# Re-ordering the stretch between two images in a two-layer state-space kernel: loads of x, token copies, first scalings, decays and planner ranks

## The chip, the cores and the metric

The kernel runs on one core of a Trainium2 chip, as one launch. The metric is the device time of that launch in microseconds (us), where less is better. Three runs of the kernel before gave 22851.89, 22874.44 and 22874.82 us, so the median is 22874.44 us.

## The reference, cut to what matters

The input is eight images of 64 x 64 positions with 192 channels, float32. Two residual layers follow each other. Layer 0 is a convolution, a chunked state-space block and an MLP; the change leaves its code alone. Layer 1 is what the change is about:

```
x = x + L1(groupnorm(x))
L1:  xz = x @ in_proj.T ; xc, z = split(xz)                 # 192 -> 2 x 384 channels
     xc = silu(depthwise_conv3x3(xc) + b)
     xs = [rows, columns, rows reversed, columns reversed]  # K = 4 directions, L = 4096 steps each
     dt, B, C = split(x_proj @ xs) ; delta = softplus(dt_proj @ dt + bias)
     h[t] = exp(delta*A) * h[t-1] + (delta*u) * B           # 384 channels x 16 states
     y[t] = sum_n h[t] * C ; y += D * xs
     y = layernorm(sum of the four directions) * silu(z) ; out = y @ out_proj.T
```

## The kernel before, in words

Layer 0 runs over all eight images first. Layer 1 then runs image by image. One image has two parts.

**The scan** (`main`, L1891) is the long part. It takes 32 steps (4 directions x 8 chunks of 512 tokens), and each step has 24 units (8 pairs of states x 3 channel tiles of 128). A unit needs `ea` (ScalarE's exponentials of the decay, `decay`, L1735, read from `dr`, the repeated delta), `g` (TensorE's transposes of `pw`, `supply`, L1747, where `pw` is ScalarE's scaling of `duT` by B, `weigh`, L1720), two VectorE scans (`run`, L1775) and GpSimd's product with `cb`, the repeated C. TensorE sums `hs` into `y` (L1813), and VectorE adds `y` to `yacc` once per channel tile and step (L1824). For the state pairs from p = 4 on, the first 128 columns of `g` are not transposed from `pw` but multiplied with `dg`, a diagonal matrix that is built in DRAM: a small strided write into `dz` (L1624) and then a load of `dg` (L1625). The order of pairs is 0, 4, 1, 5, ..., so the fourth unit of an image is the first that needs `dg`.

**The boundary** between two images does three things at once. It finishes the image that was just scanned (`finish`, L1354): mean and variance by TensorE (`p_m`, `p_v`, L1366), centring (L1378) and scaling (L1423) on VectorE, the gate `z` (reload x as `xa2`/`xb2`, multiply with the scaled weights `wza`/`wzb`, silu, product at L1498), the output projection `p_o` (L1517, L1529), the addition to x (L1543) and the store. The four token groups of x go through two buffers of `xa2`/`xb2`, so the third and the fourth group can only be loaded once the first and second have been stored. It also prepares the next image (`front`, L1157): load x as `xa1`/`xb1` in four groups, project it (`p_x`, L1150 and L1151), copy it into a bordered tile `pad` (L1215), convolve with nine taps in 3 channel tiles x 2 halves (ScalarE the first tap, `begin`, L1241; VectorE the other eight, `convolve`, L1257, 48 instructions of 128 x 2048), silu, and store three layouts: `xo0` by rows (L1282), `xo1` by columns through the transposing copy `xt` (L1296, L1303), and `xo2` by tokens (`by_tokens`, L1309: TensorE transposes `p_xq`, copies `xq`, stores). Last comes the prologue of the next scan (`prologue`, L1839, and `prologue_of`, L1873): load the first chunk `xc` and `ut` (L1591, L1595), project it (`p_d`, L1610), copy to `xdbl` (L1617), softplus (`spa`, L1652), `de` (L1658), the repeated `dr` (L1709), `duT` (L1674), ten first scalings `pw` and two first decays `ea`.

The nine boundaries (before the first image, seven between images, after the last) are not written out by hand. Each is planned by `Flow` (L105): generators yield steps with an engine, a cost and an earliest start; `Flow.run` always takes the step with the smallest planned start plus 0.01 x the rank of its generator (`RANKS`, L43), and `Flow.keep` ties each engine's instructions to the order so found. So costs and ranks in the text are not times: they decide in which order each engine issues. The order on an engine is then fixed. TensorE, VectorE, ScalarE and the DMA queue of SyncE each work it off in that order, and a waiting instruction holds what stands behind it. In the built program each DMA issue also waits for the landing of the DMA eight places before it in SyncE's queue.

Of the kernel before, what the change touches and what calls it, by code (L numbers as in the profile page):

```python
# [40 lines left out]
BIG = 60.0  # L41

RANKS = dict(  # L43
    begin=-31, fill=-131, enter=-89, load=-44, store=-81, convolve=-1, prologue=-61, project=-11, product=-20, norm=-22,
    square=-24, silu=-131, centre=-36, gate=-94, weights=285, drift=8,
)
# [1000 lines left out]
def layer1(tc, consts, x1s, mv1, out, w_in, w_x, w_dt, w_out):  # L1047
# [7 lines left out]
    with ExitStack() as ctx:  # L1055
# [67 lines left out]
        def scaled(wa, wb, b, half):  # L1123

            cols = slice(half * DIN, half * DIN + DIN)
            load = lambda: [
                nc.sync.dma_start(out=wa, in_=w_in[:C1, cols]),
                nc.sync.dma_start(out=wb[:C2], in_=w_in[C1:, cols]),
                nc.sync.dma_start(out=wb[C2:], in_=w_in[C1:, cols]),
            ]  # L1130
            r = yield step("SP", 0.3, load)
            r += 3
            for w, g in ((wa, sca), (wb, scb)):
                r = yield step(
                    "ACT", 0.5, lambda: [nc.scalar.activation(w, w, AF.Copy, scale=g[:, b : b + 1])], r
                )
            return r
# [19 lines left out]
        def front(f, cx, cx2, mq, b, xo):  # L1157
# [19 lines left out]
            def enter():  # L1177
                yield from scaled(wxa, wxb, b, 0)
                for d in range(DT):
                    for g in range(NG):  # L1180
                        yield "wait", ("xl", g)
                        ps = []
                        for i in range(2):
                            yield "take", "mm"
                            ps.append(mq.tile([128, TT], F32, name="p_x1", tag="mm"))
                        got["ps", d, g] = ps
                        f.at["ps", d, g] = yield step(
                            "PE", 2.6, lambda: from_pair(ps, wxa, wxb, xas[g], xbs[g], slice(d * 128, d * 128 + 128))
                        )
# [57 lines left out]
            def convolve():  # L1247
                for d in range(DT):
                    for h in range(2):
                        yield "wait", ("begun", d, h)  # L1250
                        xs, r = got["xs", d, h], f.at["begun", d, h]
                        for j in range(1, 9):
                            r = yield step(
                                "DVE",
                                2.24,
                                lambda: [
                                    nc.vector.scalar_tensor_tensor(  # L1257
                                        xs, tap(d, h, j), kw[:, d, j : j + 1], xs, ALU.mult, ALU.add
                                    )
                                ],  # L1260
                                r - f.LAG,
                            )
                        f.at["conv", d, h] = r
                    f.give("pad", r)
# [5 lines left out]
            def store():  # L1270
                for d in range(DT):
                    yield "take", "xt"
                    xt = gp.tile([128, WI, HI], F32, name="xt1")
                    for h in range(2):
# [14 lines left out]
                        if h == 0:  # L1289
                            seeded(q + 3)  # L1290
                        f.fork(by_tokens(d, h, xs, r))
                        r = yield step(
                            "ACT",
                            3.7,
                            lambda: [
# [13 lines left out]
            def by_tokens(d, h, xs, r):  # L1309
                xf = xs.rearrange("p h w -> p (h w)")  # L1310
                for e in range(2):
# [31 lines left out]
                    q = yield step("SP", 0.1, lambda: [nc.sync.dma_start(out=dst, in_=xq)], q)  # L1343
                    f.give("xq", q + 3)
                    if g == 0:
                        seeded(q + 3)
# [7 lines left out]
        def finish(f, cx, mq, b):  # L1354
# [62 lines left out]
            def scale(t, yv, rs, r):  # L1417
                for d in range(DT):
                    r = yield step(
                        "DVE",  # L1420
                        0.62,
                        lambda: [
                            nc.vector.scalar_tensor_tensor(  # L1423
                                yv[:, d], yv[:, d], v["gam"][:, d : d + 1], rs, ALU.mult, ALU.mult
                            )
                        ],
                        r - f.LAG,
                    )
# [3 lines left out]

            def load(gs):
                for g in gs:
                    yield "take", "xl2"
                    xa = fp.tile([C1, 2, TT], F32, name="xa2", bufs=2)
                    xb = fp.tile([128, TT], F32, name="xb2", bufs=2)
                    got["xl2", g] = xa, xb
                    r = yield step("SP", 0.3, lambda: pair_of(xa, xb, x1s[b], g))
                    f.at["xl2", g] = r + 3  # L1440

            def weights():
                f.at["wz"] = yield from scaled(wza, wzb, b, 1)

            def gate(gs):
                yield "wait", "wz"
                for g in gs:
# [3 lines left out]
                    for d in range(DT):  # L1451
# [3 lines left out]
                        for i in range(2):  # L1455
# [4 lines left out]
                            "PE",  # L1460
                            2.6,
                            lambda: from_pair(ps, wza, wzb, xa, xb, slice(d * 128, d * 128 + 128)),
# [24 lines left out]
            def product(gs):  # L1487
                for g in gs:
                    yield "rank", RANKS["product"] + g * RANKS["drift"]
                    yield "wait", ("ln", g)  # L1490
                    for d in range(DT):
# [3 lines left out]
                            "DVE",  # L1495
                            1.15,
                            lambda: [
# [51 lines left out]

            ts, gs = range(NT), range(NG)  # L1550
            gens = (project(gs), product(gs), norm(ts), square(ts), silu(gs), centre(ts), gate(gs), weights(), load(gs))
            return [(gen, RANKS[gen.__name__]) for gen in gens]

# [10 lines left out]
        def scan(xo):  # L1564
# [154 lines left out]

            def weigh(s, p, j, i):  # L1720

                st = state[s]
                if i == 0:
                    st["pw", p, j] = pools["pw1"].tile([128, 2 * DT, 2, 64], F32, name="pw")
                n = 2 * p + i
                o(
                    nc.scalar.activation(  # L1727
                        st["pw", p, j][:, :, i],
                        st["duT"][:, j].rearrange("p (g c) -> p g c", c=64),
                        AF.Copy,  # L1730
                        scale=st["bt"][:, j, n : n + 1],
                    )
                )

# [104 lines left out]
            def prologue(f, mq, cx_b, cx_a):  # L1839
# [23 lines left out]
                for name, n in (("pw1", 8), ("bc1", 3), ("e1", 3)):  # L1863
                    spool(name, n)
                load_c(0, ORDER[0])
                for d in range(DT):
                    yield "wait", ("du", d)
                for t in todo[:10]:
                    yield step("ACT", 0.55, lambda: weigh(*t), f.free["ACT"])
                for u in range(2):  # L1870
                    yield step("ACT", 1.35, lambda: decay(u), None, "explog")

            def prologue_of(f, d):  # L1873
# [8 lines left out]
                f.give("tmp", r)  # L1882
                yield step("SP", 0.1, lambda: repeat_delta(0, d), r)
                yield "take", "mm"
# [40 lines left out]
            def chains(f, mq, cx_b, cx_a):  # L1925
                f.pool("tmp", 2)
                return [(prologue(f, mq, cx_b, cx_a), RANKS["prologue"])] + [
                    (prologue_of(f, d), RANKS["prologue"]) for d in range(DT)
                ]
# [3 lines left out]
        for b in range(nb + 1):  # L1933

            f = Flow(tc, after=True)
            f.STAY = 0.0
            keeper.append(f.keep)
            mq_x, fr_x, fq_x, fi_x = ExitStack(), ExitStack(), ExitStack(), ExitStack()
# [123 lines left out]
```

## Time and profile before

| what | value |
|---|---|
| median of three runs | 22874.44 us |
| the profiled execution: its own time, its span | 22840.11 us, 22838.4 us |
| busy share of the span: TensorE, VectorE, ScalarE, GpSimd | 94%, 93%, 87%, 70% |
| mean granted TensorE clock | 0.976 |
| first scan of the first image starts; last scan of the eighth ends | 4958.7 us; 22715.2 us |
| seven boundaries between last and first scan, each | 212.1, 212.2, 215.7, 216.7, 212.9, 215.3, 218.9 us |
| stretch after the last scan | 123.2 us |

The view of stretches gives, for each window of the execution (us from the span's start), each engine's busy time with its number of instructions, then the granted TensorE clock, the mean busy share of the 16 DMA engines and the rate in GB/s. The timeline lists instructions in order of time: start, duration, engine, line, operation, output<-inputs, shape, how many were merged, and in brackets how long the engine was idle just before, and whose end it waited for. SPq is SyncE issuing a DMA; its duration is the issue and not the transfer. A line of the view of waits names who waited for whom, the total, how often, and the longest.

### The profile page before, as it was taken

How to read it: one execution, taken by the hardware profiler on the slowest of the kernel's cores; microseconds unless marked ns; L12 is line 12 of the kernel's file. 1: busy time of each engine (PE TensorE's matmuls, PEld its weight loads, DVE VectorE, ACT ScalarE, POOL GpSimd, SP SyncE). 2: the span in 40 equal slices, each digit the busy share in tenths (PEclk: the TensorE clock that was granted, in tenths of full speed). 3: DMA queues.
4: the chain of work that ended last, by engine and by line, in shares of the span. 5: the costliest groups of instructions: out<-in, count | busy, mean ns of one | idle time of the engine just before them, and what ended most of it. 6: DMA issues, size and time to landing. Idle time of an engine off the chain costs nothing.

```text
span 22838.4 us, 348211 instructions
## 1 busy us (share of the span) xinstructions
PE 21469.6 (94%) x118788; PEld 10895.2 (48%) x118788; DVE 21138.2 (93%) x22413; ACT 19918.9 (87%) x35288; POOL 16095.4 (70%) x12872
## 2 busy tenths in 40 slices
PE   8999999979999999999989999999999999999999
PEld 4444444435554555455545554554455445544554
DVE  7888888869998999899989998999899999999998
ACT  6666666669998999899989998999899989988998
POOL 1111111139995999599959995999599869987997
PEclk8999999989999999999999999999999999999999
DMA  2111111133333333333333333333333333333333
GB/s 53 46 45 42 46 46 46 39 89 92 93 93 109 93 93 95 106 92 95 93 108 93 94 89 111 92 96 85 114 93 93 88 114 93 93 85 114 93 93 79
DMA packets 1706715, 1954.31 MB, mean 86 GB/s; under 512 B 538112, under 2 KB 1039776, under 8 KB 1695712
## 3 DMA queue, kind: packets, MB, share of 16 engines
q1 hardware_dynamic: 1704928, 1932.03, 31.2%
q8 instruction: 933, 15.29, 0.3%
q14 instruction: 854, 7.00, 0.1%
HBM read 1316.16 MB, written 212.60 MB: 67 GB/s over the span
## 4 chain that ended last, share of the span: by engine, by line
PE 47%; ACT 24%; DVE 10%; POOL 8%; issue 5%; DMA 4%; SPq 2%; DVEq 0%; POOLq 0%; ACTq 0%
ACT ea L1742 11%; ACT pw L1727 10%; PE y L1813 10%; PE g L1768 10%; POOL hs L1798 7%; DVE hs L1784 3%; PE g L1756 3%; PE p_f L970 3%; PE p_d L1610 2%; PE p_x L463 2%; PE p_f L990 2%; DMA dr<-de 2%; PE p_dt L1645 2%; PE p_o L887 2%; PE p_y L804 1%
## 5 line engine op out<-in xcount | busy, mean ns | idle before, releaser
L1798 POOL TENSOR_TENSOR hs<-hs,cb 128x1024 f32<-128x1024 f32 x6144 | 14577.3, 2373 | 501.7 <-DMA dr<-de 5.6
L1784 DVE TENSOR_TENSOR_SCAN hs<-ea,cy,g 128x512 f32<-128x512 f32 x10752 | 12900.7, 1260 | 186.2 <-PE g L1768 167.2
L1742 ACT ACTIVATE ea<-dr,an 128x512 f32<-128x512 f32 x12288 | 8140.7, 710 | 431.2 <-DVE hs L1784 399.8
L1727 ACT ACTIVATE pw<-duT,bt 128x384 f32<-128x384 f32 x14336 | 7833.5, 601 | 15.9 <-DVE duT L1674 15.9
L1813 PE MATMUL y<-hs,sel 128*64 128x512 f32 x24576 | 6632.6, 618 | 357.5 <-POOL hs L1798 338.2
L1768 PE MATMUL g<-ident,pw 128*128 128x128 f32 x43008 | 6094.4, 281 | 50.6 <-DVE hs L1784 13.4
L1768 PEld LDWEIGHTS g<-ident,pw 128*128 128x128 f32 x43008 | 4612.4, 141 | 2533.8 <-issue 1232.4
L1796 POOL COPY cy<-hs 128x2 f32<-128x2 f32 x6144 | 1151.6, 187 | 1979.0 <-DVE hs L1784 1933.4
L1756 PEld LDWEIGHTS g<-dg,duT 128*64 128x64 f32 x24576 | 1556.5, 136 | 2065.9 <-issue 1493.8
L1756 PE MATMUL g<-dg,duT 128*64 128x128 f32 x24576 | 2257.8, 282 | 180.6 <-DVE hs L1784 106.2
L1813 PEld LDWEIGHTS y<-hs,sel 128*64 128x64 f32 x24576 | 1234.2, 135 | 1559.2 <-issue 869.4
L1784 DVE TENSOR_TENSOR_SCAN hs<-ea,g 128x512 f32<-128x512 f32 x1536 | 1751.9, 1198 | 149.5 <-PE g L1768 93.9
L380 POOL TENSOR_TENSOR s<-xs 96x512 f32<-96x512 f32 x64 | 116.3, 1817 | 2130.4 <-DVE xs L358 1841.7
L1257 DVE SCALAR_TENSOR_TENSOR xs<-pad,p,xs 128x2048 f32<-128x2048 f32 x384 | 900.1, 2349 | 150.2 <-ACT xs L1241 141.3
L1645 PE MATMUL p_dt<-xdbl,wd 13*128 13x512 f32 x1536 | 865.1, 644 | 98.0 <-DVE duT L1674 71.8
L1610 PE MATMUL p_d<-xc,wx 128*44 128x512 f32 x1536 | 796.9, 602 | 73.2 <-DMA xc<-xo 73.2
L380 POOL TENSOR_TENSOR s<-sq 96x512 f32<-96x512 f32 x128 | 182.5, 1426 | 938.5 <-ACT sq L393 822.6
L970 PE MATMUL p_f<-h,wf 96*128 96x512 f32 x1536 | 757.0, 631 | 43.9 <-ACT zs L565 27.4
L358 DVE SCALAR_TENSOR_TENSOR x<-xx,p,x 96x512 f32<-96x512 f32 x1024 | 783.8, 815 | 15.2 <-ACT x L347 15.0
L358 DVE SCALAR_TENSOR_TENSOR xs<-xin,p,xs 96x512 f32<-96x512 f32 x1024 | 746.7, 769 | 3.6 <-ACT xs L347 3.6
L990 PE MATMUL p_f<-m,wf 128*96 128x512 f32 x1536 | 692.9, 601 | 0.0
L1667 PEld LDWEIGHTS p_du<-ident,de 128*128 128x128 f32 x3072 | 322.7, 141 | 610.5 <-DVE de L1658 408.8
(213 smaller groups left out, 19352.5 us busy)
## 6 DMA issues: line engine op xcount, KB each, us to landing
cb<-cd SPq DMA_DIRECT2D x4096, 128.0 KB
dr<-de SPq DMA_DIRECT2D x3072, 128.0 KB
xc<-xo SPq DMA_DIRECT2D x256, 768.0 KB
dg<-dz SPq DMA_DIRECT2D x256, 512.0 KB
e<-csd SPq DMA_DIRECT2D x256, 384.0 KB
ut<-xo SPq DMA_DIRECT2D x128, 768.0 KB
ut<-xo SPq DMA_DIRECT2D x256, 384.0 KB
xo<-xs SPq DMA_DIRECT2D x48, 1024.0 KB
```

Source lines behind the costliest of these rows:

```text
L358: nc.vector.scalar_tensor_tensor(im(out[:, ct]), tap(ct, j), w[:, ct, j : j + 1], im(out[:, ct]), ALU.mult, ALU.add)
L970: nc.tensor.matmul(ps, wf1[:, ct, mt * 128 : mt * 128 + 128], h[:, ct], start=ct == 0, stop=ct == 1)
L1610: nc.tensor.matmul(st["p_d"][:44], wx[:, d, k], st["xc"][:, d], start=d == 0, stop=d == DT - 1)
L1645: nc.tensor.matmul(ps, st["wd"][32:45, d * 128 : d * 128 + 128], xds[s % 2][32:45], start=True, stop=True)
L1727: nc.scalar.activation(st["pw", p, j][:, :, i], st["duT"][:, j].rearrange("p (g c) -> p g c", c=64), AF.Copy, scale=st["bt"][:, j, n : n + 1],
L1742: nc.scalar.activation(ea[:, f], state[s]["dr", d][:, f], AF.Exp, scale=an[:, k, p, at : at + 1])
L1756: nc.tensor.matmul(gs[f][i * 64 : i * 64 + 64, j * 128 : j * 128 + 128], state[s]["duT"][:, j, (2 * d + f) * 64 : (2 * d + f) * 64 + 64], ...
L1768: nc.tensor.transpose(gs[f][:, j * 128 : j * 128 + 128], state[s]["pw", p, j][:, 2 * d + f].rearrange("p a b -> p (a b)"), ident,)
L1784: nc.vector.tensor_tensor_scan(rev(h[:, f]), rev(ea[:, f]), rev(g[f]), 0.0 if first(s) else state[s - 1]["cy"][:, p, d, f : f + 1], ALU.mu ...
L1796: o(nc.gpsimd.tensor_copy(st["cy"][:, p, d], h[:, :, last]))
L1798: o(nc.gpsimd.tensor_mul(h, h, bc(st["cb", p], 1, [128, 2, TT])))
L1813: o(nc.tensor.matmul(y[half[f]], sel, hc[:, f], start=p == ORDER[0] and k > 0, stop=p == ORDER[-1]))
```

## The change

The planner's numbers change (`RANKS` for every generator; the costs of `p_x` and `p_z` steps 2.6 to 2.95, a tap 2.24 to 2.36, and small ones). Beyond that:

```diff
+DRAIN = 8.5, 9.0
 # scaled():
-            r += 3
+            r = max(r, DRAIN[0] * half) + 3
 # store(): the column copy waits until the first token store of its half is planned
                         f.fork(by_tokens(d, h, xs, r))
+                        yield "wait", ("tokens", d, h)
                         r = yield step("ACT", 3.75, ... nc.scalar.copy(xt...) ...)
 # by_tokens():
                     f.give("xq", q + 3)
+                    if e == 0:
+                        f.at["tokens", d, h] = q
 # finish(): load() becomes fetch(), and it and weights() wait for the front's last load of x
+                    if b < nb - 1:
+                        yield "wait", ("xl", NG - 1)
-                    f.at["xl2", g] = r + 3
+                    f.at["xl2", g] = max(r, DRAIN[0]) + 3
 # weigh() can run on VectorE
+                if vector:
+                    o(nc.vector.tensor_scalar_mul(to, what, by))
+                else:
+                    o(nc.scalar.activation(to, what, AF.Copy, scale=by))
 # prologue(): four of the first ten scalings go to VectorE, the two first decays get a chain of their own
-                for t in todo[:10]:
-                    yield step("ACT", 0.55, lambda: weigh(*t), f.free["ACT"])
+                for n, t in enumerate(todo[:10]):
+                    if n < 8 and t[3]:
+                        yield step("DVE", 0.5, lambda: weigh(*t, True), at)
+                    else:
+                        yield step("ACT", 0.55, lambda: weigh(*t), at)
+            def prologue_decays(f):
+                yield "wait", "spools"
                 for u in range(2):
+                    yield "wait", ("dr", u)
                     yield step("ACT", 1.35, lambda: decay(u), None, "explog")
 # the boundary's planner
             f.STAY = 0.0
+            if b:
+                f.free["PE"], f.free["DVE"] = DRAIN
```

The scan's own loop is the same. The instructions of a boundary are the same in number and kind, but for the four scalings that change engine and for fewer switches of ScalarE's function table; their order on each engine is another.

## The prediction

> **What bounds the kernel now.** I read the page first (VectorE and TensorE are 93% and 94% busy, so a mean says little), then the stretches. The code that changes runs only in the boundaries:
>
> ```profile
> core 0: us, PE busy (x) PEld busy (x) DVE busy (x) ACT busy (x) POOL busy (x), PEclk, DMA share, GB/s
> ...
> 11475.20:11690.90 215.70, 182.87 (x536) 71.84 (x536) 169.05 (x116) 133.90 (x146) 6.25 (x9) 0.92 0.44 142
> ...
> 22715.20:22838.40 123.20, 115.24 (x300) 43.43 (x300) 55.16 (x59) 47.34 (x57) 5.42 (x5) 0.96 0.19 55
> 4790.00:4958.70 168.70, 76.15 (x259) 41.69 (x258) 119.28 (x67) 86.74 (x91) 1.79 (x5) 0.66 0.52 164
> ```
>
> Seven such boundaries, the first and the last make 1796 us, 8% of the span. In a middle one VectorE works 169 of 216 us, so about 47 us are to be had, and no more. To see where they are I read VectorE's timeline of the boundary at 11475, counting from T = 11482.8, where TensorE's last `y` ends:
>
> ```profile
> 11482.91 0.69 DVE L1824 TENSOR_TENSOR yacc<-yacc,y 128x512 f32<-128x512 f32 x1 [2.77 <-PE y L1813]
> ...
> 11507.93 23.79 DVE L1257 SCALAR_TENSOR_TENSOR xs<-pad,p,xs 128x2048 f32<-128x2048 f32 x10 [15.89 <-ACT xs L1241]
> ...
> 11628.10 33.26 DVE L1257 SCALAR_TENSOR_TENSOR xs<-pad,p,xs 128x2048 f32<-128x2048 f32 x14
> ...
> 11672.29 0.68 DVE L1617 COPY xdbl<-p_d 44x512 f32<-44x512 f32 x1 [6.36 <-PE p_d L1610]
> ...
> 11690.90 1.22 DVE L1784 TENSOR_TENSOR_SCAN hs<-ea,g 128x512 f32<-128x512 f32 x1 [2.63 <-DMA xo<-xq]
> ```
>
> The taps begin at T+25 and end at T+178.5, VectorE being nearly full between; the first chunk is in `xdbl` from T+189.5; the scan starts at T+208. The start is late because of SyncE:
>
> ```profile
> SPq L1146 <- PE y L1813: 17.5, 1, 17.5
> ```
>
> The first load behind `wxb` is `xa2` of the finishing image, whose memory is freed by the last `y`. It waits 17.5 us, and the loads of the next image's x stand behind it; the one that the first taps need is the fifth pair of six.
>
> The first scan is not the end of the boundary. The fourth unit waits for `dg`:
>
> ```profile
> 11702.56 1.12 PE L1756 MATMUL g<-dg,duT 128*64 128x128 f32 x8 [8.16 <-DMA dg<-dz]
> ```
>
> so it scans only at 11704.56 (T+221.7), after 5.48 us of idle VectorE. From there on nothing depends on the boundary: in each of the seven, the 25th unit follows the fourth by 58.8 to 59.4 us. So I measure a boundary by its fourth unit. Read alike in all seven timelines, the means are: taps T+25.8 to T+177.7, `xdbl` T+187.1, first scan T+207.2, fourth unit T+219.6 (215.2 to 223.1).
>
> **What the Trainium skill says.** "DMA: Bandwidth & Descriptors", section "Issuing engines are not separate DMA queues": all DMAs share the same 16 engines. The trace agrees: from 11673 to 11703 their mean share is near 0.9 at 200 to 437 GB/s, so order decides what lands when. Its section "Two DMAs through the same engine are not ordered" has a dependent DMA issued only after the first one's semaphore; here `dg` waits for `dz` (3.4 us where nothing else is in the way, 11718.77). "TensorE: Matmul & The Clock Gate", section "What's actually happening": after an idle window of about 3.4 us TensorE runs at half clock; the trace grants 0.50 at 11667, and `p_d` costs 3.61 + 1.10 us there, twice its warm price. "ScalarE: Activation LUTs", section "What ACT_TABLE_LOAD costs": 1283 ns plus a drain; the trace has 1.28 us.
>
> **The change, part by part,** for a middle boundary, in the order that the built program issues.
>
> *Loads of x first.* The four pairs follow `wxb` at once; what they wait for is work of the scan long done. So they issue from 11465.4. 3.1 MB at the 270 GB/s of 11486 to 11501 is 12 us plus some 2 of latency, so they land by 11480, behind the last products. Then TensorE sets the start: a cold group (3.57 + 1.12 = 4.7, as at 11496.96) and two of 2.97 give T+10.7. But ScalarE's queue now has the scaling of `wza` and `wzb` between the first group's pads and the second's. The last boundary has just this order of loads, and its scalings start at 22732.72 and 22733.65, T+9.9 and T+10.8; they are done at T+11.4. Behind them stand four pads of 0.63 and the first tap's 2.1: T+16.1 instead of 25.8, 9.7 us earlier. Without the scalings it would be T+14.2, so this wait costs 1.9.
>
> *Two centrings moved.* Before, two of 1.7 us ran in the idle start; now the first comes after nine taps. That is 3.4 us more between the first and the last tap; all other counts up to the last tap stay (48 taps, 18 scalings, 9 products, 6 additions). The stretch was 151.9 us, idle included, and becomes 155.3. I walked the queues for new idle: TensorE runs all twelve `p_x` groups early, which fills the eight PSUM banks, and ScalarE waits with the third tile's pads for tap 16; but five centrings' means are ready when VectorE asks. One product waits about 3 us for the third reload of `xa2`, as large as the waits it replaces (4.92 at 11551.7). Taps end at T+171, 6.7 us earlier. Bounds: 0 to 10 earlier.
>
> *Tokens ahead of the column copy.* The first chunk needs `xo0` and the first token store of the third tile. Their transposes stand on TensorE behind `p_z` of the fourth group, whose `xa2` is stored and reloaded (8.6 us at 11597.49, 12.2 at 11625.61 with `xo1` in front). The last addition before it falls at T+145, so `p_z` starts at 154 to 157; 3 us, two transposes, two copies, the 3.8 us column copy, two more copies and the store bring the load of `xc` to T+166. It lands 8.1 later (11658.28), and a cold `p_d` of 4.7 gives `xdbl` at T+178, 9.1 us earlier.
>
> *From `xdbl` to the fourth unit* was 32.5 us. Now three products (1.2 each) stand before `de`, and the column copy (3.8) has moved between the second and third softplus, so the third `de` comes about 13.5 us after `xdbl` instead of 8.5. More important, SyncE's order ends with eight `dr`, `xo1`, three stores, `xo2`, two `cb`, four `dr`, three stores, and only then `dz` and `dg`; before, `dz` was ahead of `cb`. The bytes from `dr` to the last store are 1.05 + 2.1 + 0.79 + 0.52 + 0.26 + 0.52 + 0.79 = 6.0 MB. At 280 GB/s with `xo1` at 437 that is 19 us; `dr` begins 8 us after `xdbl`, add 1.7 of latency and 1 for slow issue: 30. `dg` lands 5 later, and TensorE needs 2: 37 us, 4.5 more than before. The first boundary, which has `dz` last already, took 32.2 with 1.5 MB less (5.4 us): 37.6. So the fourth unit comes at T+215, a gain of 4.6.
>
> *First scalings and decays.* Ten scalings took ScalarE 5.17 us. Six take 3.1; VectorE's four cost 0.40 each (128x192 takes 0.30, 128x128 0.27); bounds 0.27 to 0.69. The first scan may start 6 to 10 us earlier, but it is followed by the wait for `dg`, so I count nothing; if `dg` were early, some 3 us.
>
> *Table loads.* ScalarE switches four times less, 5.1 us; it is not the bound, so zero. If it were late at the third softplus, one switch would be worth 1.3.
>
> *First boundary:* the end is the same `dr`, `dz`, `dg`; `xc` is earlier, but its use waits for the last tap: 1 us gained (0 to 3). *Last:* TensorE is 115 of 123 us busy and does the same work; `ysq` now stands behind the scalings, and a product ends nearer the end: 1 us lost (-2 to 4).
>
> Sum: 7 x 4.6 + 1 - 1 = 32 us. The profiled execution of 22840.1 becomes 22808. The median lies 34 us above that execution, and the runs scatter by 23, so I carry the difference over: 22874.4 - 32 = 22842.
>
> **Rivals.** *The whole head start arrives.* If `dg` lands 32.5 us after `xdbl` as before, each boundary gains 9.1, 64 us: 22811. For it: 30 us of the DMA's work is an estimate. Against: `dz` last. *The end swallows it.* If the end takes 41.6 us, the gain is nil: 22874; the same comes if the loads don't issue early, against which the built waits speak. *Slower:* SyncE's queue at the end, with place and price: the 6.0 MB run at 0.19 MB/us instead of 0.28 (199 and 215 GB/s stand at 11685 to 11691, where `dr` and `cb` with their small rows dominate), and `xo1` loses its higher rate. Then they take 31.6 us instead of 19, the end 49.6 and a boundary 8.0 us more: 7 x 8.0 = 56, 22930. It turns the sign from an end of 41.6 us on.
>
> **How the numbers follow.** Forecast 0.42, whole gain 0.30, swallowed 0.18, slower 0.10. A change under 0.2% (46 us) is about what a measurement here can't tell from none. Faster than that: 0.26 from the whole gain, 0.15 from the forecast's upper part, 0.41; slower 0.08, from the last; the same 0.51. The range goes from 84 us faster (12 per boundary, all bounds of the start well used) to 16 us slower, 22790 to 22890; the forecast's own is 22815 to 22865. Both sides of the sign lie in it because seven repeated ends multiply each us of error.
>
> **What would show it.** Right: loads of `xa` issued some 17 us before the last `y` ends; first tap near T+16 behind ScalarE's scalings; last tap near T+171; `xdbl` near T+178; first scan near T+198; VectorE idle over 10 us before the fourth unit, released by `dg`, at T+215. Wrong: taps interrupted by idle TensorE or ScalarE stretches, or `dg` landing within 33 us of `xdbl`, or beyond 42.

## The result, and the profile after

| | median | lowest to highest | runs |
|---|---|---|---|
| kernel before | 22859.61 us | 22838.03 to 22878.45 | 11 |
| kernel after | 22806.38 us | 22793.09 to 22824.09 | 11 |

The ratio is 0.9977, with a 95% interval of 0.9968 to 0.9986: 53 us faster, 0.23%, with 32 to 73 in the interval. The three runs that the prediction starts from had a median 15 us above the one that stands here.

The profiled execution of the kernel after took 22798.87 us, with a span of 22797.2 and a mean TensorE clock of 0.975. The view of stretches, for the same three stretches as before (the middle boundary is now at T = 11485.8):

```profile
core 0: us, PE busy (x) PEld busy (x) DVE busy (x) ACT busy (x) POOL busy (x), PEclk, DMA share, GB/s
11479.10:11684.86 205.76, 182.46 (x536) 71.86 (x532) 170.35 (x119) 127.28 (x139) 5.35 (x7) 0.93 0.42 139
22670.00:22797.20 127.20, 116.38 (x300) 43.09 (x300) 55.97 (x59) 45.62 (x56) 5.40 (x5) 0.97 0.19 53
4807.70:4976.40 168.70, 74.34 (x252) 39.68 (x253) 119.13 (x63) 84.01 (x86) 0.48 (x2) 0.66 0.53 165
```

VectorE does the same work in the middle boundary, 170 us (169 before), in 10 us less. The last boundary is 4 us longer. VectorE's and TensorE's timeline of the middle boundary, in the places shown of the kernel before:

```profile
11485.83 0.69 DVE L1831 TENSOR_TENSOR yacc<-yacc,y 128x512 f32<-128x512 f32 x1 [1.87 <-PE y L1820]
...
11501.63 7.21 DVE L1259 SCALAR_TENSOR_TENSOR xs<-pad,p,xs 128x2048 f32<-128x2048 f32 x3 [15.12 <-ACT xs L1243]
...
11660.10 0.68 DVE L1626 COPY xdbl<-p_d 44x512 f32<-44x512 f32 x1 [2.79 <-PE p_d L1619]
...
11684.86 6.78 DVE L1791 TENSOR_TENSOR_SCAN hs<-ea,g 128x512 f32<-128x512 f32 x6 [2.92 <-DMA xo<-xq]
...
11696.60 1.12 PE L1763 MATMUL g<-dg,duT 128*64 128x128 f32 x8 [8.29 <-DMA dg<-dz]
...
11698.60 2.33 DVE L1791 TENSOR_TENSOR_SCAN hs<-ea,g 128x512 f32<-128x512 f32 x2 [6.96 <-PE g L1775]
```

The first tap starts at T+15.8, the copy of the first chunk into `xdbl` at T+174.3, the first scan at T+199, and the fourth unit, after 6.96 us of idle VectorE, at T+212.8. The fourth unit still waits for `dg`, in all seven boundaries. The wait of SyncE's queue for the last `y` hasn't gone, but now it stands behind the loads of the next image, as its timeline shows (start, duration of the issue):

```profile
11468.36 0.58 SPq L1148 DMA_DIRECT2D xa<-x  x1
...
11474.45 2.80 SPq L1148 DMA_DIRECT2D xb<-x  x2
11485.86 0.33 SPq L1148 DMA_DIRECT2D xa<-x  x1
```

The load at 11485.86 is the finishing image's; before, it was the one at the head.

Means over the seven middle boundaries, read from the timelines as in the prediction, T being the end of TensorE's last `y`. A tap counts from its start (the first) or to its end (the last), `xdbl` is the start of the copy into it, and the fourth unit the start of its first scan:

| | first tap | last tap | xc issued | xdbl | first scan | fourth unit | xdbl to fourth |
|---|---|---|---|---|---|---|---|
| before | 25.8 | 177.7 | 173.8 | 187.1 | 207.2 | 219.6 | 32.5 |
| forecast | 16.1 | 171 | 166 | 178 | 198 | 215 | 37 |
| after | 15.4 | 169.0 | 161.9 | 173.6 | 198.2 | 211.6 | 38.0 |

By the fourth unit a boundary gains 8.0 us; the seven gains scatter, and the standard error of their mean is 1.6. From the 25th unit to the end of an image's scan both kernels take 1960 us; at the 25th unit the gain is 8.6, over seven boundaries 60.2. In the two profiled executions 4.0 are lost at the end, and 15.6 before the 25th unit of the first image. So 60.2 - 4.0 - 15.6 = 40.6 of the spans' 41.2. Of the 15.6, 16.0 stand already at the end of layer 0, whose code is the same, and some 0.5 are won back. TensorE's granted clock in the first 600 us was 0.88 in the kernel before and 0.85 in the kernel after. I count the 16.0 as no part of the change, because e5 below, which has nearly all of the change, was granted 0.88 and ended layer 0 as early as the kernel before.

### The profile page after: what moved, and what is told of

Its sections match the earlier page's. It is cut to its first block, busy times and chain, and to the rows that moved or that the text cites. A ratio compares the mean times of both kernels' runs of the same rounds, so it can differ in the third digit from the quotient of the medians.

```text
span 22797.2 us, 348200 instructions
## 1 busy us (share of the span) xinstructions
PE 21475.4 (94%) x118788; PEld 10903.6 (48%) x118788; DVE 21149.8 (93%) x22445; ACT 19859.8 (87%) x35227; POOL 16101.6 (71%) x12872
## 5 line engine op out<-in xcount | busy, mean ns | idle before, releaser
L1740 ACT ACTIVATE pw<-duT,bt 128x384 f32<-128x384 f32 x14304 | 7817.3, 601 | 19.4 <-DMA xo<-xt 19.4
L382 POOL TENSOR_TENSOR s<-xs 96x512 f32<-96x512 f32 x64 | 121.7, 1901 | 2138.7 <-DVE xs L360 1849.4
```

The costliest lines, as they stand in the source:

```text
L1740: o(nc.scalar.activation(to, what, AF.Copy, scale=by))
```

## The experiments

My theory was that the early loads of x make the gain, and that SyncE's queue, in which `dz` and `dg` stand last, takes part of it back at the end. The rivals were the order of tokens and ranks, and the shared scalings and early decays. In the table T+ are means over the seven middle boundaries of one profiled execution.

| run | first tap | xdbl | first scan | fourth unit | median, us | ratio to before, 95% interval |
|---|---|---|---|---|---|---|
| kernel after | 15.4 | 173.6 | 198.2 | 211.6 | 22806.38 | 0.9977, 0.9968 to 0.9986 |
| e1_loads_alone | 18.0 | 179.4 | 199.3 | 211.2 | 22803.22 | 0.9979, 0.9971 to 0.9988 |
| e2_loads_back | 27.6 | 185.7 | 210.6 | 224.2 | 22884.16 | 1.0016, 1.0009 to 1.0023 |
| e3_copy_back | 15.6 | 175.9 | 194.8 | 208.1 | 22771.02 | 0.9968, 0.9955 to 0.998 |
| e4_dz_early | 15.6 | 173.4 | 198.2 | 208.6 | 22773.02 | 0.9968, 0.9955 to 0.998 |
| e5_scalings_back | 15.3 | 173.2 | 198.1 | 211.2 | 22799.04 | 0.998, 0.9971 to 0.9988 |
| e6_wz_later | 13.8 | 172.2 | 197.0 | 210.4 | 22781.81 | 0.9974, 0.9964 to 0.9984 |
| e7_copy_dz | 15.4 | 175.9 | 196.4 | 206.3 | 22761.91 | 0.9964, 0.9951 to 0.9976 |
| e8_copy_dg | 15.4 | 175.9 | 198.3 | 206.5 | 22750.20 | 0.996, 0.9947 to 0.9974 |
| e9_last_copy_back | 15.4 | 173.3 | 201.5 | 208.9 | 22770.91 | 0.9963, 0.9951 to 0.9976 |
| e10_combined | 13.5 | 171.5 | 198.9 | 205.7 | 22766.34 | 0.9961, 0.9948 to 0.9975 |
| e11_prologue_back | 15.6 | 173.7 | 199.9 | 212.3 | 22799.94 | 0.9977, 0.9968 to 0.9986 |
| e12_numbers_alone | 26.3 | 182.6 | 204.1 | 213.4 | 22808.67 | 0.9982, 0.9974 to 0.999 |

The kernel before was run anew beside each group of experiments, with medians from 22846.61 to 22850.05, so times are compared by the ratios. Their intervals are as wide as 30 to 60 us and tell apart only the large steps. The finer ones are read from the fourth unit, where 1 us stands for 7. There the difference between a run and the kernel after, boundary by boundary, has a standard error of 0.6 to 1.2 us, so a difference of 1 us isn't shown by one of these means.

**The loads alone (e1) and the change without them (e2).**

```diff
 # e1: the kernel before, with this in finish()'s load() and weights(); e2: the kernel after without it
+                    if b < nb - 1:
+                        yield "wait", ("xl", NG - 1)
```

> The kernel before with one thing added: the finishing image's reloads and gate weights are planned behind the next image's last load of x. T is the end of TensorE's last y of a boundary; kernel before: first tap T+25.8, first chunk in xdbl T+187.1, fourth unit T+219.6; kernel after: T+15.4, T+173.6, T+211.6. My theory (the early loads carry the gain, and the end of the boundary stays as in the kernel before, 32.5 us from xdbl to the fourth unit): first tap near T+16, xdbl near T+178, fourth unit near T+211, so about 60 us less than before, no worse than the kernel after. Rival (the tokens ahead of the column copy and the new ranks carry it): the taps start early, but xdbl comes at T+184 or later, the fourth unit at T+216 or later, and less than 25 us is gained.

> The kernel after without its two waits for the next image's last load, so that the reload of the finishing image's x stands first in SyncE's queue again. My theory: the first load waits some 17 us for the last y again, first tap at T+24 to T+26, xdbl near T+183, the end of the boundary keeps its 38 us from xdbl to the fourth unit, which comes near T+221: the time is that of the kernel before within 15 us, or above it. Rival (order of tokens, ranks, scalings carry the gain): the fourth unit stays at T+215 or earlier and at least 30 us of the 53 are kept.

Both came out for the theory. The ratio of e1 stands for 48 us, where 60 were expected. With the loads alone the fourth unit stands at T+211.2, 8.4 us earlier than before, as in the kernel after, and the end keeps its length (31.9 from `xdbl`). Without the loads the change is slower than the kernel before, by 4.6 us a boundary, and SyncE's first load waits for the last `y` again (24.1 us in the boundary at 11511). But e2 doesn't bring back the order of the kernel before. In its timeline two pairs of the finishing image stand even ahead of `wxa` and `wxb`, and `wza` and `wzb` ahead of three pairs of the next image (`fetch` has a rank of its own in the change, -116). So e2 isn't the change minus one thing; e12 below has the old order. In e1 the first tap is 2.6 us later than in the kernel after. VectorE's timeline of e1 shows what it does there instead (T = 11492.7):

```profile
11496.12 1.75 DVE L1378 TENSOR_TENSOR yacc<-yacc,p_m 128x1536 f32<-128x1536 f32 x1 [2.63 <-PE p_m L1366]
11498.70 1.75 DVE L1378 TENSOR_TENSOR yacc<-yacc,p_m 128x1536 f32<-128x1536 f32 x1 [0.82 <-PE p_m L1366]
11510.69 4.82 DVE L1257 SCALAR_TENSOR_TENSOR xs<-pad,p,xs 128x2048 f32<-128x2048 f32 x2 [10.24 <-ACT xs L1241]
```

TensorE makes two `p_m` first, and the two centrings run in VectorE's idle start; in the kernel after they come among the taps, and VectorE is idle for 15.12 us instead. So the last tap is only 1.8 us apart in the two kernels.

**The column copy back (e3).**

```diff
 # the kernel after, store()
-                        yield "wait", ("tokens", d, h)
```

> The kernel after without the wait of the column copy for the first token store of its half. My theory: taps start and end as in the kernel after (T+15.4, T+169); the load of xc is issued some 4 us later (a column copy of 3.8 us stands before the token copies), xdbl near T+178; but that shortens the end by as much as it lengthens the start, since SyncE's queue then has the same bytes in front of dg: fourth unit within 2 us of T+211.6, the time within 15 us of the kernel after. Rival (tokens first is worth its full 4 us): fourth unit at T+215 or later, the time 25 us or more above the kernel after.

Neither: the fourth unit comes 3.5 us earlier than in the kernel after (standard error 1.2). `xdbl` is 2.3 later, but from there to the fourth unit it takes 32.2 us instead of 38.0. The fourth unit waits for `dg` in all seven boundaries of both kernels, after 6.6 and 6.5 us of idle VectorE, so SyncE's queue moved it. First the kernel after (T = 11485.8):

```profile
11667.83 5.15 SPq L1718 DMA_DIRECT2D dr<-de  x8
11673.08 0.53 SPq L1306 DMA_DIRECT2D xo<-xt  x1
...
11678.09 3.74 SPq L1724 DMA_DIRECT2D cb<-cd  x2
11681.92 3.10 SPq L1718 DMA_DIRECT2D dr<-de  x4
...
11687.33 0.48 SPq L1633 DMA_DIRECT2D dz<-xdbl  x1
11691.56 0.38 SPq L1634 DMA_DIRECT2D dg<-dz  x1
```

then e3 (T = 11475.5):

```profile
11663.72 7.54 SPq L1717 DMA_DIRECT2D dr<-de  x12
...
11673.38 0.48 SPq L1632 DMA_DIRECT2D dz<-xdbl  x1
11677.70 0.38 SPq L1633 DMA_DIRECT2D dg<-dz  x1
```

In the kernel after the first `dr` is issued some 6 us earlier, but the store of `xo1`, three stores of the finished image, a token store and two `cb` then stand between the eighth and the ninth `dr`. From the first `dr` to `dz` it takes 19.4 us there. In e3 these had gone out before, and it takes 9.8. So `dz` and `dg` are issued some 3.5 us earlier.

The first scan moves too (T+194.8 for T+198.2), by other waits. ScalarE's timeline has one of them, in the kernel after:

```profile
11666.78 3.75 ACT L1299 COPY xt<-xs 128x2048 f32<-128x2048 f32 x1
...
11670.91 0.59 ACT L1661 ACTIVATE spa<-p_dt 128x512 f32<-128x512 f32 x1
...
11679.90 3.15 ACT L1740 ACTIVATE pw<-duT,bt 128x384 f32<-128x384 f32 x6 [3.67 <-DMA xo<-xt]
```

and in e3, where the last column copy runs ahead of all softplus:

```profile
11663.98 0.58 ACT L1660 ACTIVATE spa<-p_dt 128x512 f32<-128x512 f32 x1
...
11668.64 3.13 ACT L1739 ACTIVATE pw<-duT,bt 128x384 f32<-128x384 f32 x6
```

In the kernel after the third softplus stands behind the column copy, and the store of `xo1` that follows the copy is issued behind eight `dr`. The pool of the first scalings is opened where the pool that holds `xt` is closed, and the trace has them waiting for that store's landing until 11679.90. In e3 the store went out earlier, and they don't wait. The first scan itself then waits for the landing of a token store in the kernel after, in five boundaries of seven (2.92 us in the one shown above), and in e3 in none.

**`dz` early (e4), then `dg` too (e7, e8).**

```diff
 # e4: the kernel after; e7: without the tokens' wait too
                 r = yield step("DVE", 0.7, ready["keep"])
+                state[0]["write"]()     # the DMA into dz; spread() then only loads dg for s = 0
 # e8: as e7, and
-                ready["spread"]()       # from main()
+                ready["spread"]()       # to prologue(), ahead of load_c(0, ORDER[0]); pool dg1 opened there
```

> The kernel after, with the small write into dz issued right behind the store of cd at the beginning of the prologue instead of behind everything; dg stays last in SyncE's queue. My theory (dz and then dg, last in the queue, end the boundary): the issue of dz (0.5 us) and the wait for its landing (3.7 us) disappear in front of dg, the fourth unit comes 4 us earlier, near T+207.5, and the time falls by 28 us, to about 22778. Rival (the bytes in front of dg fill the DMA engines, so that dg lands no earlier; or the next bound, ScalarE's scalings behind the first decays, takes over): the fourth unit moves by less than 1.5 us and the time by less than 10 us.

The fourth unit came 3.0 us earlier instead of 4 (standard error 1.0), so the theory holds. SyncE's waits in the kernel after have `dg` held by `dz` with the line

```profile
SPq L1634 <- DMA dz<-xdbl: 3.7, 1, 3.7
```

and in e4 there is no such line. That the dependent DMA is issued only when the first has landed is what the Trainium skill, "DMA: Bandwidth & Descriptors", section "Two DMAs through the same engine are not ordered", asks for; 3.7 us is its price here, paid only because both stood last. Earlier in the queue `dz` isn't free either: the issue of `xo0` behind it takes 1.9 to 2.6 us instead of 0.4, but there SyncE waits for the token copy and for `de` anyway.

> The kernel after without the wait of the column copy for the tokens and with dz written at the beginning of the prologue. Alone, the first gave a fourth unit at T+208.1 and 22771, the second T+208.6 and 22773, where the kernel after has T+211.6 and 22806. Theory (two separate delays: the third softplus and the scalings behind the column copy, and dz's write and landing in front of dg): they add, fourth unit near T+205, 22745 to 22750. Rival (one delay, the end of SyncE's queue, seen twice, or ScalarE's first scalings as the next bound): the fourth unit stays at T+207 or later, 22762 or more.

> As the run before this one, with the load of dg also issued early, ahead of the first cb and of the twelve dr. Theory (nothing but dg holds the fourth unit): it follows the first scan by some 7 us instead of 13, at T+203, 22735; its 0.5 MB ahead of dr make the first scan up to 2 us later. Rival (the DMA engines are full there, so that dg in front only pushes dr and the first scan back): the fourth unit within 1 us of the run before this one.

e7 lies between its two expectations: of 3.5 and 3.0 us, 5.3 come together (standard error 0.8). e8 agrees with the rival: with `dg` early the fourth unit is where it was, at T+206.5. VectorE's timeline of e8 (T = 11454.0):

```profile
11651.17 6.78 DVE L1795 TENSOR_TENSOR_SCAN hs<-ea,g 128x512 f32<-128x512 f32 x6 [4.64 <-PE g L1779]
11659.16 2.33 DVE L1795 TENSOR_TENSOR_SCAN hs<-ea,g 128x512 f32<-128x512 f32 x2 [1.22 <-PE g L1779]
```

The fourth unit hardly waits any more (1.22 us, for `g` from `pw`), but the first scan comes 1.9 us later than in e7: what was a wait for `dg` is now a wait ahead of the first scan. ScalarE shows the cause:

```profile
11646.92 0.72 ACT L1753 ACTIVATE ea<-dr,an 128x512 f32<-128x512 f32 x1 [5.41 <-DMA dr<-de]
11647.86 0.72 ACT L1753 ACTIVATE ea<-dr,an 128x512 f32<-128x512 f32 x1 [0.22 <-DMA dr<-de]
11648.49 3.13 ACT L1744 ACTIVATE pw<-duT,bt 128x384 f32<-128x384 f32 x6
```

The decays that the change has put early wait for `dr`, which land later with the 0.5 MB of `dg` ahead of them, and the scalings stand behind them. The expectation had this cost at up to 2 us.

**Scalings (e5), and scalings and decays (e11), as before.**

```diff
 # e5: the kernel after
-                        yield step("DVE", 0.5, lambda: weigh(*t, True), at)
+                        yield step("ACT", 0.55, lambda: weigh(*t), at)
 # e11: the kernel after with the kernel before's code for the scalings and decays of the prologue
```

> The kernel after with all ten first scalings on ScalarE; the planner then also puts the write into dz ahead of the first cb in SyncE's queue, dg staying last. The kernel after has the first scan at T+198.2 and the fourth unit at T+211.6. My theory (the scalings are off the path, since the fourth unit waits for dg): first scan up to 2 us later, fourth unit no later than T+211.6, and up to 3 us earlier through dz: 22785 to 22810. Rival (VectorE's share in the scalings carries part of the gain): first scan and fourth unit both at least 2 us later, 22820 or more.

> The kernel after with the first scalings and the two first decays as in the kernel before: ten scalings on ScalarE, and the decays behind them; the planner also puts dz ahead of the first cb. Theory (the fourth unit waits for dg): the first scan comes 2 to 4 us later, the fourth unit within 1 us of T+211.6, the time within 8 us of the kernel after. Rival (scalings and decays carry part of the gain): fourth unit 2 us later or more, 15 us or more in the time.

No effect of either part on the fourth unit is seen: it moves by -0.4 and +0.7 us (standard error 0.9 each), the first scan by -0.1 and +1.7. One of VectorE's scalings took 0.42 us, as counted. But the place of `dz`, which moves in both as a side effect, has to be looked at, or it could hide a loss. SyncE's timeline in e5:

```profile
11658.67 1.54 SPq L1633 DMA_DIRECT2D dz<-xdbl  x1
11660.30 5.25 SPq L1724 DMA_DIRECT2D cb<-cd  x1
```

In the kernel after, in the lines shown at e3, the first of the two `cb` took 1.47 us to issue, and 4.2 lie between the issues of `dz` and `dg`. In e5 the wait for `dz` is gone, but the issue right behind `dz` takes 5.25 us. The one loss makes up for the other, `dg` is issued 0.8 us earlier in the mean, and so a hidden loss through the scalings is not larger than some 2 us.

**ScalarE's scalings of the gate weights behind the pads (e6).**

```diff
 # the kernel after, weights()
                 if b < nb - 1:
-                    yield "wait", ("xl", NG - 1)
+                    yield "wait", ("pad", 0, 2)
```

> The kernel after with the scaling of wza and wzb planned behind the pads of the third group of the first tile, where the kernel after has it in front of the second group's pads. My theory (ScalarE's wait for wza's load costs the start 1.9 us): first tap near T+13.5 instead of T+15.4, last tap and fourth unit 1.9 earlier, 13 us less in the time. Rival (VectorE, or the products that wait for z, absorb it): first tap earlier, last tap within 0.7 us of the kernel after, the time within 6 us.

First tap 1.6 us earlier (standard error 0.4), last tap 1.4 (0.5), fourth unit 1.2 (0.7): the wait was real at the taps. The time can't show 1.2 us a boundary. In the kernel after ScalarE's timeline has it between the first group's pads and the second's:

```profile
11490.62 1.27 ACT L1217 ACTIVATE pad<-p_x,gb 128x512 f32<-128x512 f32 x2 [18.16 <-PE p_x L1153]
11496.19 0.61 ACT L1137 ACTIVATE wza<-wza,sca 128x384 f32<-128x384 f32 x1 [4.31 <-DMA wza<-in_w_in]
```

**Only the last column copy back (e9), and three edits together (e10).**

```diff
 # e9: the kernel after, store(); e10: with the edits of e4 and e6 too
-                        yield "wait", ("tokens", d, h)
+                        if (d, h) != (DT - 1, 1):
+                            yield "wait", ("tokens", d, h)
```

> The kernel after, but the last column copy of a boundary (third tile, second half) doesn't wait for the tokens; the other five do. The planner then puts the last column copy and the store of xo1 ahead of the softplus and of all twelve dr, and dz ahead of cb. The kernel after has xc issued at T+161.9, xdbl T+173.6, fourth unit T+211.6; the run with all six copies back has T+165.1, T+175.9, T+208.1. Theory (what the tokens cost is the last copy alone: it holds the third softplus and the store of xo1, whose landing frees the memory of the first scalings; what they bring is the early xc): xdbl stays near T+173.6, the end shrinks from 38 to 33 us, fourth unit near T+206.5, 22770. Rival (the same bytes leave through the same DMA engines, so that an earlier xc only waits longer for dg): fourth unit at T+208 or later, no better than all six copies back.

> The kernel after with three edits: the last column copy doesn't wait for the tokens, dz is written at the beginning of the prologue, and the scaling of wza and wzb is planned behind the third group's pads. Theory (early xc 2.3 us, dz early 1.8 to 3.0, earlier taps 1.2, added to the T+208.1 of all copies back): fourth unit near T+203, so about 60 us less than the kernel after, 22745. Rival (from T+206 on the bytes of the boundary set the end, as where dg was issued early without a gain): fourth unit at T+205.5 or later, 22762 or more.

My theory fell in both, the early `xdbl` and the short end didn't come together. In e9 `xdbl` is at T+173.3 as expected, but the fourth unit only at T+208.9. It is not the rival's cause either: the fourth unit doesn't wait there. ScalarE's and VectorE's timeline of e9 (T = 11475.1):

```profile
11669.21 0.72 ACT L1750 ACTIVATE ea<-dr,an 128x512 f32<-128x512 f32 x1 [5.95 <-DMA dr<-de]
...
11672.52 0.72 ACT L1750 ACTIVATE ea<-dr,an 128x512 f32<-128x512 f32 x1 [0.48 <-DMA dr<-de]
11673.15 3.13 ACT L1741 ACTIVATE pw<-duT,bt 128x384 f32<-128x384 f32 x6
...
11675.82 9.24 DVE L1792 TENSOR_TENSOR_SCAN hs<-ea,g 128x512 f32<-128x512 f32 x8 [6.54 <-PE g L1776]
```

Four decays now stand ahead of the scalings, each waiting for a `dr`. The column copy stands ahead of the first softplus, so the first `de` begins 5 us later after `xdbl` than in the kernel after (12.2 us for 7.0). The first `dr` is issued even 10 us later after `xdbl` (18.1 for 7.7), because three stores, a token store, `dz` and two `cb` now stand ahead of it in SyncE's queue, and the `cb` behind `dz` takes 2.9 us to issue in this boundary. The first scan comes at T+201.5, 3.3 us later than in the kernel after, and then eight scans run with hardly a gap. In e10 it is the same: the first scan waits 6 to 7 us for `g`, the fourth unit for nothing. By the fourth unit e10, e7 and e8 are the fastest kernels here, at T+205.7 to T+206.5. They lie too close to say which is best; all three beat the kernel after by some 5 to 6 us a boundary.

**The planner's numbers alone (e12).**

```diff
 # the kernel before with the kernel after's RANKS (load=12 for both loads) and the costs of its steps
```

> The kernel before with the ranks and step costs of the kernel after and nothing else of the change: the loads keep their old order in SyncE's queue. Theory (new ranks alone don't start the boundary earlier, and they gather all twelve dr and two stores at the end of SyncE's queue): first tap at T+24 or later, fourth unit at T+219.6 or later, the time that of the kernel before or up to 35 us more. Rival (the fit of the ranks carries much of the gain): fourth unit at T+216 or earlier, 25 us less or better.

The theory fell. With the old order of loads and a first tap at T+26.3 a boundary gains 6.2 us, and the ratio, 0.9982, stands for 41. VectorE's waits in the middle boundary show where. The kernel before:

```profile
DVE xs L1257 <- ACT xs L1241: 15.9, 1, 15.9
DVE yacc L1378 <- PE p_m L1366: 9.9, 3, 4.9
DVE xdbl L1617 <- PE p_d L1610: 6.4, 1, 6.4
```

and e12:

```profile
DVE xs L1257 <- ACT xs L1241: 17.9, 1, 17.9
DVE de L1658 <- ACT spa L1653: 4.7, 2, 4.3
DVE yacc L1378 <- PE p_m L1366: 3.5, 2, 2.7
```

The centrings wait 6.4 us less, and the 6.4 for `xdbl` are gone, since `xc` is issued at T+164.4, 9.4 us earlier: in the new order of SyncE's queue it stands behind one token store of the third tile, before behind two. `xdbl` itself comes only 4.5 us earlier, since its copy stands behind other work on VectorE (11674.03 to 11681.60 in this boundary). New waits of 4.7 for the softplus take part of it back.

## Why the prediction was right, by its own steps

*Loads of x first* was right, in size too: issued 17.2 us before the last `y` ends, first tap T+15.4 for T+16.1. e6 puts the wait for ScalarE's scalings at 1.6 us; the prediction has 1.9. e1 shows that this part alone is worth what the whole change is worth.

*Two centrings moved:* from the first to the last tap it takes 153.6 us, forecast 155.3, before 151.9. The last tap is at T+169.0 instead of T+171.

*Tokens ahead of the column copy* is the term that was mis-sized: `xc` is issued at T+161.9 and not at T+166. The last addition ends at T+143.0 (forecast 145), the reload of `xa2` takes 3.5 us to its issue and 4.1 to `p_z`, 7.6 where I had counted 9 to 12 from two rows of the kernel before, and from `p_z` to the load of `xc` it takes 11.3 (forecast 10.5). From `xc` to `xdbl` it is 11.7 (forecast 12). So `xdbl` stands 4.4 us ahead of its forecast.

*From `xdbl` to the fourth unit:* 38.0 for 37, by the path that was named. In the mean the first `dr` is issued 7.7 us after `xdbl` (forecast 8) and `dg` 31.0 after it (forecast 30); TensorE uses it 5.0 later (5), and the scan follows 2.0 after that (2). The order of SyncE's queue is the one that was listed, `xo1` behind eight `dr` and `dz` last. e4 prices `dz` in front of `dg` at 3.0 us, and e3 the tokens' part of that order at 3.5; together they make 5.3 (e7). What the prediction didn't see is the scalings' wait for the store of `xo1`; it moves the first scan, not the fourth unit. Its two entries on the tokens, 2.4 us gained at `xdbl` and 4.5 lost at the end, already made this part a loss of 2.1 us a boundary; e3 has 3.5, with a standard error of 1.2. So the change gains although this part of it costs.

*First scalings and decays:* zero was right as far as e5 and e11 can tell, to some 2 us. *Table loads:* they fell from 11 to 7 a boundary, as counted. No run changed them alone, so the zero there isn't shown.

*First and last boundary:* 0.6 us gained for 1 (from the first tap to the fourth unit 149.1 us, before 149.6); 4.0 lost for 1, at the edge of the bounds given. The stretch after the last scan took 123.2 us before, 121.7 in e1 and 124.2 in e12, but 126.2 to 129.7 in the kernel after and e2 to e11. So the early loads make nothing of the 4.0 and the ranks and costs of e12 some 1.0; which other part makes the rest wasn't tried.

*The sum:* 7 x 8.0 + 0.6 - 4.0 = 53, forecast 32, measured 53 (32 to 73). That sum and measurement agree to the microsecond is chance: the 8.0 has a standard error of 1.6, which is 11 us over seven boundaries, and counted at the 25th unit the sum is 57. Of the 36 us between 22842 and the median measured, 21 are this difference, and 15 the base, three runs whose median lay higher than that of the later eleven. The rival in which the whole head start arrives was nearer in size (64), but not in its cause: the end did get 5.5 us longer, and the start shorter still. The term for `xdbl` was off by 4.4 us a boundary, nearly as much as the 4.6 that were forecast as the gain, so it is in part luck that the size came out no worse.

*Readings that don't hold as written.* The DMA engines' mean share from 11673 to 11703 in the kernel before is 0.84, and one slice in it (11691 to 11694) has 0.39 at 94 GB/s; near 0.9 holds for the others in the main. And `p_d` isn't at twice its warm price: 4.7 us there, 2.74 in e12 (at 11669.41, at a granted clock of 1.00). The drain that the prediction names beside ACT_TABLE_LOAD isn't in the trace: in 321 of the 375 loads of the kernel after, 1.3 us lie between the end of the instruction before the load and the start of the one after it. The 4.7 itself was read rightly, and none of the three moved the sum.

*What the prediction left out:* the ranks as a part of their own. Alone they gain 6.2 us (e12), the loads alone 8.4 (e1), and the change without the tokens' wait 11.5 (e3). The first two gain in different places. e1 starts the taps 7.8 us earlier and leaves the rest nearly as it was: 152.8 us from the first to the last tap, before 151.9, and an end of 31.9, before 32.5. e12 starts them no earlier, but its taps take 148.8 us and its end some 31. The kernel after has the early start and loses the other gain: its taps take 153.6 and its end 38.0. One reason is in the traces: the two centrings that run in VectorE's idle start in the kernel before, in e1 and in e12 don't run there in any of the other kernels. The planner's new `DRAIN`, which lets VectorE's plan begin at 9.0, may be why; it wasn't tried alone. The early loads and the ranks with nothing else weren't run together, so it is open whether both gains can be had.

The change without the loads (e2) is 10.7 us a boundary slower than the ranks alone. By the table 1.3 of it is the later first tap, 4.9 the longer stretch to the last tap and 7.6 the longer end, less 3.1 between the last tap and `xdbl`. If the tokens' wait and the late `dz` cost there what they cost in e3 and e4, they explain 6.5; that they do isn't shown. Why SyncE's queue in e5 needs 5.25 us behind `dz` and in the kernel before only some 3 stays open too.

## What to carry to other kernels

Where engines work off orders that a planner wrote, a DMA issue that waits for a buffer belongs behind the issues that wait for nothing, and a write that is read back through DRAM belongs where its landing is covered and nothing urgent is issued right behind it. The first edit gained 8.4 us a boundary alone. The second gained 3.0 in e4 and nothing that could be seen in e5 and e11, where `cb` stood right behind it. An order that starts one chain earlier is to be priced at both ends: the copy that gave way to the tokens came back in front of the third softplus, and its store in SyncE's queue ahead of the last `dr`, `dz` and `dg`. And when the last wait is removed, look at what the engine has queued behind the next one: decays put early hold the scalings as soon as `dr` is late.

## What the runs showed of the hardware

The write into `dz` moves 8 x 128 single elements of 4 bytes, and keeps the queue longer than its own 0.3 to 2.0 us of issue. In the ten kernels where another issue than `dg` follows it, that issue was stretched in each boundary: `cb` to 2.9 to 3.9 us (before, e1, e9, e12) and 4.2 to 6.2 (e5, e11), `xo0` to 1.7 to 2.6 (e4, e10), a token store to 1.3 to 3.2 (e7, e8). Where `dz` stands elsewhere, the first `cb` took 0.6 us in the middle boundary of e3 and 1.5 in that of the kernel after, and `xo0` 0.4 in the latter. In the other four kernels `dg` follows `dz` and waits for its landing. I had costed `dz` by its bytes, at nothing. The Trainium skill has a reason to look for ("DMA: Bandwidth & Descriptors", section "Rules for kernel authors": a strided last dimension becomes one descriptor per element), but no run here changed the number of elements, so the cause is argued and not shown.

That moving `dg` to the front gains nothing over `dz` early agrees with nearly full DMA engines at the end, which all queues share (the Trainium skill, "DMA: Bandwidth & Descriptors", section "Issuing engines are not separate DMA queues"). In e8, in the 12 us up to the first scan, the view of stretches has mean shares of 1.04 and 1.00 (its sums can come out a little above 1):

```profile
11640.00:11646.00 6.00, 5.42 (x27) 2.32 (x25) 5.59 (x12) 1.47 (x3) 0.00 (x0) 1.00 1.04 284
11646.00:11652.00 6.00, 2.46 (x10) 1.79 (x11) 1.36 (x2) 4.86 (x9) 0.00 (x0) 0.85 1.00 272
```

And the start of a launch doesn't repeat to better than some 30 us here. TensorE's granted clock over the first 600 us was 0.88 in three of the fourteen profiled executions (before, e5, e8) and 0.85 in eleven. Layer 1's first write of `pad`, which follows the same layer 0 in all of them, came at 4783 to 4791 us in the three and at 4796 to 4812 in the eleven. Each kernel was profiled once, so it isn't known whether this belongs to the execution or to the program.
